# A two-layer graph network on one core: attention outputs made turned, and node degrees laid a target a partition by way of DRAM

## The chip, the core and the metric

The kernel runs on one core of one Trainium2 chip. The metric is device time in microseconds (us) of one execution. The core has a matrix engine (PE, whose weight loads are listed apart as PEld), a vector engine (DVE), a scalar engine (ACT), a general engine (POOL) and a queue engine (SP) that issues most of the transfers; each works through its own instructions in order, and semaphores hold one engine until another has done its part.

## The reference

There are 1250 nodes of 512 features and 20000 edges, sorted by target. Two layers, both added to `x`:

```python
h = relu(layernorm(x))
x = x + L0(h, edges)      # below
h = relu(layernorm(x))
x = x + L1(h, edges)      # sum over neighbours, two dense products with batch norm and relu

def L0(x, edges):
    xn   = batchnorm(x)
    agg  = segment_sum(xn[src], dst) / max(deg, 1)[:, None]
    conv = relu(agg @ W_conv + b_conv)
    q, k, v = heads(x @ Wq), heads(x @ Wk), heads(x @ Wv)   # the first 256 nodes, 8 heads of 64
    qf, kf = phi(q), phi(k)                                 # 256 exponential features each
    kv = kf.T @ v
    z  = 1 / (qf @ kf.sum(nodes) + 1e-6)
    attn = (qf @ kv) * z @ Wo
    return batchnorm(conv + attn[pos] + x)
```

Only the first 256 nodes have attention rows of their own; later nodes take the last one's.

## The kernel before

`tile_gnn` (L1439 on) first makes, from the sorted edges, the keys by which the adjacency matrix can be counted; then `sorted_graph` does both layers. (A second program, `any_graph`, serves unsorted edges and does not run on these inputs.)

**The opening, L1458 to L1609.** Every instruction here goes through `order(...)`, which pins it to the place where it is written. Two transfers bring the targets (`kd`, rows of 400 edges that overlap, a new row every 160) and the sources (`ks`). DVE takes a sample of `kd` (L1533) and compares it (`less`, L1528); PE sums that (`cnt`, L1538). DVE makes `begin` and `pick` (L1561, L1528). PE then picks the edges of each group of ten targets: 20 small matmuls from `ks16` and 20 from `kd16` (L1568), all into one PSUM tile `keys`. Around these `keep_up` (L1517) issues matmuls on zeros whose result nobody reads: six before `cnt`, three before the 40. `halved` (L1543) makes f16 copies of `kd` and `ks` on ACT. After the 40, DVE makes `js`, `prow` and `kcol` (L1606 to L1608), each 128x250, and ACT copies `ed.dist` (L1609).

**Layer 0, in `sorted_graph`.** The 25 `batch` steps count the adjacency matrix: `onehots` (L206) makes two one-hot tiles on DVE, `op` and `ok`, `count` multiplies them on PE (L217), ACT copies the result into `adj` (L220). Most of these instructions are not pinned: a scheduler places them by their data, so what stands late in the text may run early. While the batches are made, `beside` turns the nodes (L226), makes keys (L245), their scores (L267), their maxima on DVE (`kmx`, L334, folded into `km` and turned by PE at L352), values (L337), queries (L245 again), and on DVE the statistics `gst` (L325) and the first two normalised tiles `xn` (L289).

Then comes a loop of ten iterations (L493 to L509). Iteration i issues `query(i)`: scores on PE (L267), row maxima on DVE (L461), exponentials on ACT (L465), scale on DVE (L466). Then `product(i)`: normalised nodes times `W_conv` (L422, 8 PE instructions of 512 columns), with `hi` and `lo` halves made by ACT (L110) and DVE (L111). In iterations 2 to 7 `degrees` follows: a one-hot of 21 groups on DVE (L431), two matmuls with ones that put the degree of 210 targets on all 128 partitions (L435), a maximum and a reciprocal on DVE (L437, L438) into `rdeg`, which lies in the memory of a weight that is no longer needed. Then one `batch`; `turn(i-1)`, which transposes query features (L472) with an ACT copy (L474); and `attend(i-2)`: for two heads and two blocks of 128 features a matmul with the query features as weights and 65 columns of `kv` moving, 64 value columns and one of key sums (L482). DVE adds a constant to the key sums (L485), takes the reciprocal (L486) and scales the two heads (L489) into `ao`, nodes on partitions.

After the loop `ao` is transposed on PE (L514) with four ACT copies (L516) into `aT`, features on partitions, and multiplied by `Wo` (L521). Then the aggregation (L575) multiplies `hi` and `lo` by `adj`; DVE multiplies each result by `rdeg` (L578).

**The end of the program** is the second layer: the neighbour sum (L707), two dense products (L764) and the output.

Of the kernel before, what the change touches and what calls it, by code (L numbers as in the profile page):

```python
# [11 lines left out]
F32 = mybir.dt.float32  # L12
F16 = mybir.dt.float16
F32R = mybir.dt.float32r
I32 = mybir.dt.int32
I16 = mybir.dt.int16
AF = mybir.ActivationFunctionType
# [20 lines left out]
S = 128  # L38
# [31 lines left out]
def sorted_graph(ctx: ExitStack, tc: tile.TileContext, ed, x, n1g, n1b, n2g, n2b, wconv, bconv,  # L70
# [354 lines left out]

    rdeg = ed.wk.rearrange("p k n -> p (k n)")[:, :N]

    def degrees(g0, n):
        shape = [128, n, TG, 2]
        oh = tmp.tile(shape, F16, name="oh", tag="row")  # L430
        nc.vector.tensor_tensor(oh, ed.iok[:, :TG, :].unsqueeze(1).to_broadcast(shape),  # L431
                                ed.dist[:, g0:g0 + n].unsqueeze(2).to_broadcast(shape), ALU.is_equal)
        ps = mm.tile([128, n * TG], F32, name="mm")
        for i in range(2):
            nc.tensor.matmul(ps, ed.ones, oh[:, :, :, i].rearrange("p g t -> p (g t)"), start=(i == 0), stop=(i == 1))  # L435
        c = slice(g0 * TG, (g0 + n) * TG)
        nc.vector.tensor_scalar(rdeg[:, c], ps, 1.0, None, op0=ALU.max)  # L437
        nc.vector.reciprocal(rdeg[:, c], rdeg[:, c])  # L438

    kv = ap1.tile([128, 2, HEADS, DH + 1], F32, name="kv")  # L440
    ao = ap1.tile([128, NT, HEADS, DH], F32, name="ao")
# [34 lines left out]
    def attend(n):  # L476
        t, b = pairs[n]
        pa = mm.tile([128, 2, DH + 1], F32, name="mm")
        for i in range(2):
            hd = 2 * b + i  # L480
            for mb in range(2):
                nc.tensor.matmul(pa[:, i, :], qfTs[n][:, i, mb, :], kv[:, mb, hd, :],  # L482
                                 start=(mb == 0), stop=(mb == 1))
        z = ap2.tile([128, 2], F32, name="z")
        nc.vector.tensor_scalar(z, pa[:, :, DH], KEPS, None, op0=ALU.add)  # L485
        nc.vector.reciprocal(z, z)  # L486
        for i in range(2):
            hd = 2 * b + i
            nc.vector.tensor_scalar(ao[:, t, hd, :], pa[:, i, :DH], z[:, i:i + 1], None, op0=ALU.mult)  # L489
# [3 lines left out]
    for i in range(len(pairs) + 2):  # L493
# [7 lines left out]
        if 2 <= i < 8:  # L501
            degrees(21 * (i - 2), min(21, NGR - 21 * (i - 2)))
# [7 lines left out]
    aT = ap1.tile([128, KD, TOK], F32, name="aT", tag="tT")  # L510
    for f in range(KD):
        ps = mm.tile([128, TOK], F32, name="mm")
        for t in range(NT):
            nc.tensor.transpose(ps[:, t * 128:(t + 1) * 128],  # L514
                                ao[:, t, 2 * f:2 * f + 2, :].rearrange("p h d -> p (h d)"), ident)
        nc.scalar.copy(aT[:, f, :], ps)  # L516
# [467 lines left out]
def any_graph(ctx: ExitStack, tc: tile.TileContext, ed, x, src, dst, n1g, n1b, n2g, n2b, wconv, bconv,  # L984
# [8 lines left out]
    ident = const.tile([128, 128], F32)  # L993
    make_identity(nc, ident)
    ones = const.tile([128, 128], F32)
    nc.vector.memset(ones, 1.0)
    epsc = const.tile([128, 1], F32)
    nc.vector.memset(epsc, EPS)
# [440 lines left out]
def tile_gnn(ctx: ExitStack, tc: tile.TileContext, x, src, dst, *rest):  # L1439
# [11 lines left out]
    ed.dist = pre.tile([128, NGR, 2], I16, name="dist")  # L1451
# [6 lines left out]
    with tc.tile_pool(name="raw", bufs=1) as raw, tc.tile_pool(name="rawp", bufs=1, space=PSUM, side="right") as rawp:  # L1458

        kd, ks = (raw.tile([KS, SPAN], I32, name=name) for name in ("kd", "ks"))  # L1460
        kd16, ks16 = (raw.tile([KP, SPAN], F16, name=name) for name in ("kd16", "ks16"))
        few = E - (KP - 1) * STEP * RB

        def edges(queue, t, v, p0, p1, c0, c1):
            at = bass.AP(tensor=v.tensor, offset=v.offset + p0 * STEP * RB + c0, ap=[[STEP * RB, p1 - p0], [1, c1 - c0]])
            order(queue.dma_start(t[p0:p1, c0:c1], at))

        edges(nc.sync, kd, dst, 0, 112, 0, SPAN)
        edges(nc.scalar, kd, dst, 112, KS, 0, STEP * RB)
        edges(nc.scalar, kd, dst, 112, KP, STEP * RB, few)  # L1470
        edges(nc.scalar, kd, dst, 112, KP - 1, few, SPAN)
# [47 lines left out]
        keep_up(6)  # L1519
# [20 lines left out]
        def halved(t, t32, scale):  # L1540
# [105 lines left out]
```

## Time and profile before

| | |
|---|---|
| median of 3 runs | 375.6 us (373.75 to 375.77) |
| the profiled execution: its own time | 375.39 us |
| the profiled execution: span from first to last instruction | 373.6 us |
| busy PE / DVE / ACT / POOL | 356.9 / 235.8 / 157.0 / 35.4 us |

The chain that ended last passes the stages at these times: opening 0 to 12 us; keys, scores and queries 12 to 63; the loop 63 to 127; transposes and `Wo` 127 to 135; aggregation 135 to 182; layer norm 182 to 193; neighbour sum 193 to 241; dense products and output 241 to 373.

How to read it: an engine's busy share says how full it is, not whether it holds the end up. The chain of waits says that: it is followed back from the last instruction, at each step to what released it. A timeline row gives start, length, engine, source line, operation, the tiles written and read, partitions and columns, and how many equal instructions it stands for. PE rows count instructions: an f32 product is two of them.

### The profile page before, as it was taken

Reading aid. Unit: us, or ns where it says so; the run is one execution under the profiler, and the core shown is the slowest. Engines: PE = TensorE matmul, PEld = TensorE weight load, DVE = VectorE, ACT = ScalarE, POOL = GpSimd, SP = SyncE. Lnnn points to the kernel's source line nnn. Section 1 sums busy time; section 2 is a strip of 40 time slices with the busy share of each in tenths; the row PEclk is TensorE's granted clock in tenths of the full one; section 3 lists DMA queues with packets and bytes.
Section 4 is the critical chain, followed back from the end, with each engine's and each line's share of the span. In section 5 each row is a group of like instructions: output and inputs, shape, how many; then the busy total and the mean of one; then the engine's idle time right before and its main releaser. Section 6 shows DMA issues by size and latency. Waiting matters only on the chain.

```text
span 373.6 us, 4916 instructions
## 1 busy us (share of the span) xinstructions
PE 356.9 (96%) x1840; PEld 262.6 (70%) x1840; DVE 235.8 (63%) x585; ACT 157.0 (42%) x310; POOL 35.4 (9%) x55
## 2 busy tenths in 40 slices
PE   8799979999999999999999999999999999999981
PEld 4665555676565699998768888777777777777761
DVE  6899994648897325677888223172881788414673
ACT  5598549727574360111056503132552552122211
POOL 3100000000000005000000009620053000000000
PEclk9999999999999999999999999999999999999996
DMA  6853020000000372000000000050000000000124
GB/s 209 277 185 118 11 103 0 0 3 2 0 1 2 126 269 105 0 3 0 0 2 0 2 0 1 24 203 0 0 2 1 1 2 0 1 0 11 59 84 130
DMA packets 13285, 18.06 MB, mean 48 GB/s; under 512 B 1341, under 2 KB 6658, under 8 KB 13254
## 3 DMA queue, kind: packets, MB, share of 16 engines
q1 hardware_dynamic: 12542, 17.34, 13.7%
q8 instruction: 16, 0.26, 0.3%
q10 hardware_dynamic: 712, 0.33, 0.3%
q14 instruction: 15, 0.12, 0.1%
HBM read 15.11 MB, written 2.56 MB: 47 GB/s over the span
## 4 chain that ended last, share of the span: by engine, by line
PE 86%; DVE 9%; ACT 2%; DMA 1%; issue 1%; DVEq 0%
PE mm L764 31%; PE mm L707 12%; PE mm L575 12%; PE hw L422 10%; PE mm L245 3%; PE mm L449 2%; PE mm L521 2%; PE mm L482 2%; PE sc L267 2%; PE acc L217 2%; DVE op L206 1%; PE mm L226 1%; PE mm L701 1%; DVE kmx L334 1%; PE mm L472 1%; DVE ok L206 1%
## 5 line engine op out<-in xcount | busy, mean ns | idle before, releaser
L422 PE MATMUL hw<-wconv,xn 128*128 128x512 f32 (+1 forms) x80 | 37.1, 604 | 0.3 <-ACT adj L220 0.3
L779 ACT ACTIVATE kept<-mm,vT 128x313 f32<-128x313 f32 x36 | 18.5, 521 | 42.9 <-PE mm L764 41.8
L707 PE MATMUL mm<-hi,adj 128*128 128x512 f32 (+2 forms) x100 | 32.1, 399 | 0.5 <-DVE hi L655 0.4
L707 PE MATMUL mm<-lo,adj 128*128 128x512 f32 (+2 forms) x100 | 31.6, 394 | 0.0
L129 ACT ACTIVATE r<-mv,epsc 128x1 f32<-128x1 f32 x16 | 4.7, 292 | 61.6 <-DVE mv L128 61.6
L764 PE MATMUL mm<-hid,w 128*128 128x313 f32 x96 | 25.9, 427 | 0.0
L422 PEld LDWEIGHTS hw<-wconv,xn 128*128 128x128 f32 (+1 forms) x80 | 14.1, 187 | 16.4 <-issue 14.8
L575 PE MATMUL mm<-adj,lo 128*128 128x416 f32 (+3 forms) x120 | 25.1, 355 | 0.0
L575 PE MATMUL mm<-adj,hi 128*128 128x416 f32 (+3 forms) x120 | 25.1, 355 | 0.0
L206 DVE TENSOR_TENSOR op<-iop,prow 128x1280 f16<-128x1280 f16 (+2 forms) x27 | 20.7, 768 | 6.0 <-PE acc L217 5.6
L784 DVE TENSOR_TENSOR hid<-mm,kept 128x313 f32<-128x313 f32 x24 | 10.9, 478 | 20.4 <-ACT kept L779 16.9
L764 PEld LDWEIGHTS mm<-hid,w 128*128 128x128 f32 x96 | 18.1, 190 | 6.9
L575 PEld LDWEIGHTS mm<-adj,hi 128*128 128x128 f32 x120 | 21.9, 189 | 1.1
L575 PEld LDWEIGHTS mm<-adj,lo 128*128 128x128 f32 x120 | 21.8, 189 | 1.0
L707 PEld LDWEIGHTS mm<-hi,adj 128*128 128x128 f32 (+2 forms) x100 | 18.4, 186 | 5.8 <-DVE hi L655 1.4
L698 DVE SCALAR_TENSOR_TENSOR z<-h,e,mm 128x512 f32<-128x512 f32 (+1 forms) x10 | 7.0, 744 | 23.5 <-PE mm L707 15.7
L707 PEld LDWEIGHTS mm<-lo,adj 128*128 128x128 f32 (+2 forms) x100 | 18.5, 186 | 4.6 <-DVE lo L648 0.2
L217 PEld LDWEIGHTS <-op 128*128 128x128 f16 x250 | 13.7, 97 | 9.1 <-issue 4.7
L217 PE MATMUL acc<-ok,op 128*128 128x100 f16 x250 | 16.2, 207 | 3.3 <-DVE ok L206 2.7
L702 ACT COPY zT<-mm 128x512 f32<-128x512 f32 (+1 forms) x10 | 5.3, 582 | 29.3 <-PE mm L701 29.3
L764 PE MATMUL mm<-tz,w 128*128 128x313 f32 x64 | 17.5, 426 | 0.0
L764 PE MATMUL mm<-hid,sw 128*128 128x313 f32 x64 | 17.5, 427 | 0.0
(253 smaller groups left out, 704.6 us busy)
## 6 DMA issues: line engine op xcount, KB each, us to landing
w<-in_L_gnn_W_dram SPq DMA_DIRECT2D x2, 2048.0 KB
xs<-in_x_dram SPq DMA_DIRECT2D x1, 2304.0 KB
out_dram<-xs SPq DMA_DIRECT2D x7, 256.0 KB
wk<-in_L_gnn_Wk_dram SPq DMA_DIRECT2D x1, 1024.0 KB
x<-in_x_dram SPq DMA_DIRECT2D x1, 1024.0 KB
v<-in_L_gnn_Wv_dram SPq DMA_DIRECT2D x1, 1024.0 KB
wconv<-in_L_gnn_W_conv_dram SPq DMA_DIRECT2D x1, 1024.0 KB
wk<-in_L_gnn_Wq_dram SPq DMA_DIRECT2D x1, 1024.0 KB
```

What stands on the lines that cost most here:

```text
L206: i = nc.vector.tensor_tensor(t[:, qs], iota.unsqueeze(1).to_broadcast(shape), keys[:, bt, qs].unsqueeze(2).to_broadcast(shape), ALU.is_equal)
L217: nc.tensor.matmul(acc[:, :, q * TG:(q + 1) * TG], op[:, q, :, i], ok[:, q, :, i].rearrange("p (j t) -> p j t", t=TG), start=(q == 0 and i ...
L245: nc.tensor.matmul(ps, wt[:, k, b * 128:(b + 1) * 128], hT[:, k, :TOK], start=(k == 0), stop=(k == KD - 1))
L267: nc.tensor.matmul(ps[:, a, :M], tT[a * 64:a * 64 + 64, b, t * 128:(t + 1) * 128], projT[a * 64:a * 64 + 64, :], start=True, stop=True)
L422: nc.tensor.matmul(ps[:n], xn[:, f, :n], wct[:, f, :], start=(f == 0), stop=(f == KD - 1))
L449: nc.tensor.matmul(ps[:, i, :], kf[:, t, hd, mb * 128:(mb + 1) * 128], va[:, t, hd, :], start=(t == 0), stop=(t == NT - 1))
L482: nc.tensor.matmul(pa[:, i, :], qfTs[n][:, i, mb, :], kv[:, mb, hd, :], start=(mb == 0), stop=(mb == 1))
L575: nc.tensor.matmul(ps, part[:k, j, fs], adj[:k, j, c], start=(part is hi and j == 0), stop=(part is lo and j == NJ - 1))
L707: nc.tensor.matmul(ps[:n], adj[:k, j, t * S:t * S + n], part[:k, j, :], start=(part is hi and j == 0), stop=(part is lo and j == NJ - 1))
L764: order(nc.tensor.matmul(banks[i], left[:, k, m * 128:(m + 1) * 128], right[:, k, i * NH:(i + 1) * NH], start=(p in (1, 2, 5) and k == 0), ...
L779: nc.scalar.activation(t[:, c, :], self.A[c], AF.Identity, bias=self.part(i, 0, c)[1], scale=1.0)
L784: order(nc.vector.tensor_tensor(self.part(i, j, c)[0], self.B[c], t[:, c, :], ALU.add))
```

## The change

**Attention.** `attend` exchanges the operands. `kv` (64 columns) is the weight and the turned query features (128 columns) move, so that the result has features on partitions. The first head of a pair goes to partitions 0 to 63, the second to 64 to 127, that is, each to a half of the array's columns. The key sums get a matmul of their own for each head, with their one column repeated 64 times as weights. So there are 8 products a pair where there were 4. DVE's addition, reciprocal and scaling are now 128x128 and write `aT` directly; the transposes and copies after the loop are gone.

**Degrees.** The one-hot is the weight now and a column of ones moves: 120 targets come out on 120 partitions, one column a block, 11 blocks in three calls (iterations 2 to 4). The maxima are small, and there is a single reciprocal of 128x11. Two transfers write the 1250 values to a row in DRAM, four bytes each, and a third reads the row back onto all partitions as `rdeg`. `dist` is made again on DVE from `js` and `kcol`; the ACT copy is gone.

**The opening.** The targets come in two transfers, the first 160 columns and the 240 ahead of them, on each queue; `halved` has a third piece; the PSUM tile `keys` is two tiles; `keep_up` issues 7 and 4 instead of 6 and 3.

```diff
     rdeg = ed.wk.rearrange("p k n -> p (k n)")[:, :N]
+    dist = ap1.tile([128, NGR, 2], I16, name="dist")
+    DG = 128 // TG
+    DB = -(-NGR // DG)
+    deg = ap1.tile([128, DB], F32, name="deg")
...
+    row = dram.tile([1, N], F32, name="row")
+    nc.gpsimd.memset(deg, 1.0)
...
+        if b0 == 0:
+            nc.vector.scalar_tensor_tensor(dist, ed.js, -float(JK), ed.kcol, op0=ALU.mult, op1=ALU.add)
...
-        for i in range(2):
-            nc.tensor.matmul(ps, ed.ones, oh[:, :, :, i].rearrange("p g t -> p (g t)"), start=(i == 0), stop=(i == 1))
-        c = slice(g0 * TG, (g0 + n) * TG)
-        nc.vector.tensor_scalar(rdeg[:, c], ps, 1.0, None, op0=ALU.max)
-        nc.vector.reciprocal(rdeg[:, c], rdeg[:, c])
+        ps = mm.tile([128, n], F32, name="mm")
+        for b in range(n):
+            h0, h1 = b * DG, min((b + 1) * DG, g1 - g0)
+            w = (h1 - h0) * TG
+            for i in range(2):
+                nc.tensor.matmul(ps[:w, b:b + 1], oh[:, h0:h1, :, i].rearrange("p g t -> p (g t)"), ed.ones[:, :1],
+                                 start=(i == 0), stop=(i == 1), skip_group_check=True)
...
+        if b0 + n == DB:
+            nc.vector.reciprocal(deg, deg)
+            full, some = DG * TG, NGR // DG
+            end = full * some
+            nc.sync.dma_start(row[0, :end].rearrange("(k p) -> p k", p=full), deg[:full, :some])
+            nc.sync.dma_start(row[0, end:].rearrange("(k p) -> p k", k=1), deg[:N - end, some:])
+            nc.sync.dma_start(rdeg, row[:, :].to_broadcast([128, N]))
...
     def attend(n):
         t, b = pairs[n]
-        pa = mm.tile([128, 2, DH + 1], F32, name="mm")
-        for i in range(2):
-            hd = 2 * b + i
+        pa = mm.tile([128, 2, 128], F32, name="mm")
+        for c in range(2):
             for mb in range(2):
-                nc.tensor.matmul(pa[:, i, :], qfTs[n][:, i, mb, :], kv[:, mb, hd, :],
-                                 start=(mb == 0), stop=(mb == 1))
-        z = ap2.tile([128, 2], F32, name="z")
-        nc.vector.tensor_scalar(z, pa[:, :, DH], KEPS, None, op0=ALU.add)
+                for i in range(2):
+                    w = kv[:, mb, 2 * b + i, :DH] if c == 0 else kv[:, mb, 2 * b + i, DH:].to_broadcast([128, DH])
+                    order(nc.tensor.matmul(pa[i * DH:(i + 1) * DH, c, :], w, qfTs[n][:, i, mb, :],
+                                           start=(mb == 0), stop=(mb == 1), skip_group_check=True))
+        z = ap2.tile([128, 128], F32, name="z")
+        nc.vector.tensor_scalar(z, pa[:, 1, :], KEPS, None, op0=ALU.add)
         nc.vector.reciprocal(z, z)
-        for i in range(2):
-            hd = 2 * b + i
-            nc.vector.tensor_scalar(ao[:, t, hd, :], pa[:, i, :DH], z[:, i:i + 1], None, op0=ALU.mult)
+        nc.vector.tensor_tensor(aT[:, b, t * 128:(t + 1) * 128], pa[:, 0, :], z, ALU.mult)
...
-        if 2 <= i < 8:
-            degrees(21 * (i - 2), min(21, NGR - 21 * (i - 2)))
+        if 2 <= i < 5:
+            degrees(4 * (i - 2), min(4, DB - 4 * (i - 2)))
...
-    aT = ap1.tile([128, KD, TOK], F32, name="aT", tag="tT")
-    for f in range(KD):
-        ps = mm.tile([128, TOK], F32, name="mm")
-        for t in range(NT):
-            nc.tensor.transpose(ps[:, t * 128:(t + 1) * 128],
-                                ao[:, t, 2 * f:2 * f + 2, :].rearrange("p h d -> p (h d)"), ident)
-        nc.scalar.copy(aT[:, f, :], ps)
...
-        edges(nc.sync, kd, dst, 0, 112, 0, SPAN)
-        edges(nc.scalar, kd, dst, 112, KS, 0, STEP * RB)
-        edges(nc.scalar, kd, dst, 112, KP, STEP * RB, few)
-        edges(nc.scalar, kd, dst, 112, KP - 1, few, SPAN)
+        edges(nc.sync, kd, dst, 0, 112, 0, own)
+        edges(nc.scalar, kd, dst, 112, KS, 0, own)
+        edges(nc.sync, ahead, dst, 0, 112, own, SPAN, own)
+        edges(nc.scalar, ahead, dst, 112, KP, own, few, own)
+        edges(nc.scalar, ahead, dst, 112, KP - 1, few, SPAN, own)
...
-        keep_up(6)
+        keep_up(7)
...
-        halved(kd16, kd, 1.0)
+        halved(kd16, kd, slice(0, own), 1.0)
+        halved(kd16, ahead[:, :few - own], slice(own, few), 1.0)
+        halved(kd16, ahead[:, few - own:], slice(few, SPAN), 1.0)
...
-        keys = rawp.tile([128, 2, 2, NGR], F32, name="keys")
-        order(nc.tensor.matmul(keys, ed.ones[0:1, :], lead, start=True, stop=False, skip_group_check=True))
-        keep_up(3)
+        keys = [rawp.tile([128, 2, NGR], F32, name=f"keys{kind}") for kind in range(2)]
+        for kind in range(2):
+            order(nc.tensor.matmul(keys[kind], ed.ones[0:1, :], lead[:, kind], start=True, stop=False,
+                                   skip_group_check=True))
+        keep_up(4)
...
-        order(nc.scalar.copy(ed.dist, dist))
```

## The prediction, made before the changed kernel ran

> **What bounds the kernel now.** I read the page's busy times first, then the chain of waits in order of time, then the timeline of single stretches. The page says that PE is busy nearly throughout and that it carries most of the chain that ended last:
>
> ```profile
> span 373.6 us, 4916 instructions
> PE 356.9 (96%) x1840; PEld 262.6 (70%) x1840; DVE 235.8 (63%) x585; ACT 157.0 (42%) x310; POOL 35.4 (9%) x55
> PE 86%; DVE 9%; ACT 2%; DMA 1%; issue 1%; DVEq 0%
> ```
>
> So an edit counts where it changes PE's work, or where the 9% of DVE stand. The chain shows both kinds of place:
>
> ```profile
> 6.33 1.39 PE idle L1517 x3
> 7.73 2.98 PE keys L1568 x40
> 10.74 0.43 DVE js L1606
> 11.19 0.43 DVE prow L1607
> ...
> 37.79 0.38 DVE oh L431
> ...
> 51.97 0.61 DVE kmx L334
> 52.72 0.70 PE sc L267 x4
> ...
> 84.13 0.19 PE mm L435 x2
> ...
> 84.77 0.45 PE mm L472 x4
> 85.22 0.84 PE mm L482 x8
> 86.07 0.63 PE sc L267 x4
> 86.70 3.63 PE hw L422 x8
> ...
> 127.13 0.66 PE mm L514 x6
> 127.81 0.33 PE mm L514
> 128.14 0.65 PE mm L521 x2
> 128.90 6.48 PE mm L521 x30
> ```
>
> The reader sees four stretches: an opening in which PE and DVE alternate; 37.8 to 52.7, where DVE holds the chain (one-hots, `kmx`, statistics); the loop, PE alone, 6.2 us an iteration; and a short turn after it. DVE in the loop is the vector work that the change removes or widens:
>
> ```profile
> 85.53 1.46 DVE L438 RECIPROCAL wk<-wk 128x210 f32<-128x210 f32 x1
> 87.52 0.15 DVE L486 RECIPROCAL z<-z 128x2 f32<-128x2 f32 x1
> 88.31 0.47 DVE L489 TENSOR_SCALAR ao<-mm,z 128x64 f32<-128x64 f32 x2
> ```
>
> And the one place where two parts of the array are used by two products, the scores; a narrow window around 86.0 shows two matmuls that begin together:
>
> ```profile
> 86.00 0.49 PE L267 MATMUL sc<-projT,qT 64*128 64x256 f32 x2
> ```
>
> **The change, part by part.** All sums are made against the profiled execution, 373.6 us of span and 1.8 around it, 375.4; the median of the runs is 0.2 above that.
>
> *Opening.* `js` and `prow` now need only the first of two PSUM tiles and can run beside the 20 matmuls on `kd`; `kcol` can then follow the 40 at once, at about 10.75 and not at 11.52, where the timeline has it: -0.8. The first transfer carries 112x160 numbers and not 112x400, 105 KB less; at the 277 GB/s of the page's second slice that is 0.4 earlier, or nothing if the small transfer on ACT's queue lands last; I take -0.3. One more matmul on zeros stands before the 40; these are 0.43 apart (+0.43). The seventh before `cnt` fills a hole: six end at about 3.9, `cnt` begins at 4.48. That matters for speed: of two equal groups of 20 matmuls the first takes 1.9 (7.52 to 9.40), the second 1.1, so PE's rate doubles near 9.1, after it has been busy with hardly a hole since 4.48. If it doubles before 6.6, the 40 take 40 x 0.057 = 2.3 from `pick`'s end (6.87 less 0.3) to 8.9, and DVE's own order (statistics of `x0` to 9.16 less 0.3, then `js`, `prow`) puts `kcol` at 9.75: -1.8. If the turn stays, the three terms make -0.7. I take -1.5, nearer the first since the hole is filled; ends -1.9 and -0.3. The queue: SP issues one more transfer (0.4) ahead of `ks`, `x0` and `wk`. `x0`'s statistics end 1.5 before `js` today; `wk` is first multiplied at 15.4 and the transfers of 5 to 9 us fall off after 9. Nothing for that.
>
> *12 to 63.* As built, `dist` (like `js`, 128x250: 0.42) is early on DVE; DVE's 0.38 wait for PE at 26.25 absorbs it. The one-hots of `degrees`, scheduled at 37 today, are 960 wide and not 420. Between 420 (0.37) and `ok` of 1000 (0.67) that is 0.65, +0.28 each; the first falls into DVE's 0.35 wait before 37.79, the second does not. In the new order two more `xn` (0.26 each) stand ahead of `km`, for whose transposition (L352) PE waits, and the first scores of the queries are split in two. That is +0.28 + 0.52 + about 0.2 at 53; later ten counting matmuls (0.46) have moved ahead and the 0.26 wait for `adj` before L422 goes, against a second drain for the split scores (0.6). Net +0.8; ends 0 (this stretch gives way elsewhere) and +1.2.
>
> *Loop, attention.* Today 8 instructions in 0.84. Now 16, each with 128 moving columns; transposes of that width (L472) are 0.109 apart. If the halves run together as the scores do, 8 x 0.109 = 0.87, and a change of the array's shape: four score instructions take 0.63 where two steps of 0.216 (L521) are 0.43, so 0.2 for it. 1.05 against 0.84, +0.2 a pair, **+1.6**. If they run one after the other: 16 x 0.109 + 0.2 = 1.94, +8.8. Ends: +0.2 (no cost of the shape) and +8.8. I take the first kind since the only row with two products in parts of the array shows them side by side.
>
> The Trainium skill (TensorEngine Tiling (Array Packing), Key Properties) says that a change of tiling mode, not of tile, drains the engine. The trace agrees: the two 8-column instructions of L248 take 0.53 in the chain where full ones take 0.43. With a drain that costs nothing the whole sum would be 1.4 lower.
>
> *Loop, degrees.* Gone: 6 x 0.19 = 1.1 of PE. New: 22 matmuls of one column, each behind an f16 weight load of 120 columns. Loads of 128 f16 columns keep pace with matmuls 0.046 apart (L217); f32 ones hold L482 at 0.112. Neither has 120 columns, so the middle, 0.075: 1.65, **+0.5**; ends -0.1 and +1.3.
>
> The Trainium skill (TensorE: Matmul & The Clock Gate, Weight-path perf modes) has fast loading only for exactly 128 weights, and 1/1.2 ns a column otherwise; 120 columns would then take 100 ns, an estimate by that page, and the term would be +1.1, the whole 0.6 higher. No row here shows such a load.
>
> *Loop, DVE.* Per iteration 0.38 + 0.37 + 1.46 go in six of them. 0.10 + 0.15 + 0.47 become 0.34 + 0.95 + 0.34 (0.34 is `xn`, 128x128; 0.95 from 1.46 for 210 and 0.15 for 2). The new order holds `qf`, which waits for ACT's exponential, ahead of the next one-hots, so DVE stands some 1.1 in that wait: 5.0 of work and 1.1 make 6.1 of PE's 6.2. What waits for DVE there is the next `product`, for `lo`, with about 1.1 in hand. Nothing, but the cover is thin; without it 0.2 an iteration.
>
> *Degrees by DRAM.* The three transfers start at about 98 on SP; the first reader is L578 at 139.2. The nearest row for small packets is queue 10 on the page: 712 packets in 0.3% of 16 engines' span, 25 ns each. 1250 even through one engine are 31 us, and 640 KB at the 182 GB/s of 120 to 140 another 3.5. Covered. `xs`, next on SP, goes at 125.8 as before. POOL sets `deg` once; it is idle from 40 to 140.
>
> *After the loop.* From the last `attend` to L575 8.05 pass. Now 32 x 0.216 = 6.9, 0.2 for the shape, and a wait: the last `aT` comes 0.3 + 0.95 + 0.3 after the last product lands, while PE has six instructions that do not need it: about 0.35. **-0.6**. The four ACT copies lay on this path and are in that.
>
> Sum: -1.5 + 0.8 + 1.6 + 0.5 - 0.6 = +0.8. Time 376.1.
>
> **The rivals.**
> - *Halves one after the other* (slower). For it: 128-row products share all rows, and no row here shows two column halves. Against it: the scores. +8.8 in place of +1.6: **383.3**. It decides from the point where a pair costs 1.2.
> - *Halves together, their weight loads not hidden.* An f32 load of 64 columns, half of what holds L482 at 0.112, adds 0.055 to each step: 8 x 0.164 + 0.2 = 1.5, +5.4 in all: **379.9**.
> - *DVE's order bounds the loop*: 7 x 0.2 more, **377.5**; the sign is `lo` late for L422.
> - *Faster*: the opening's best end, the middle stretch free, 0.12 a pair, loads of 0.046, a shorter wait before `Wo`: -1.9 + 0 + 1.0 - 0.1 - 0.8 = -1.8, **373.6**. For it: DVE has 5 us of idle time after 56.5 to give back. Against it: L352 waits for DVE before that.
> - *The DRAM row late*: L578 waits, yet seven PSUM tiles stand before PE must stop. 377 and up.
>
> **How the numbers follow.** Forecast 0.42 (own range 374.0 to 377.5), one after the other 0.20, loads not hidden 0.13, DVE's order 0.08, DRAM 0.02, faster 0.15. The likeliest is 376.1. The range 373.4 to 383.5 reaches from the faster case to the serial one and leaves about half of the ends of these two, 0.15, outside. Half a percent (1.9 us) is what a measurement of this kernel can tell: faster 0.15, same 0.42, slower 0.43.
>
> **What would show it.** In the profile after: the new attention products, 16 instructions in about 1.05, with starts in twos; 22 one-column matmuls and their spacing; `kcol` near 10; L352 at 52.9 (53.4 - 1.5 + 1.0); `Wo` in 7.4. The forecast is wrong if the products start one by one 0.109 apart, if PE's rate turns after 9, or if L422 waits for DVE in the loop.

## The result, and the profile after

The changed kernel took **376.78 us** (median of 22 executions, 374.62 to 380.71), the kernel before 374.55 us (22 executions beside it, 373.06 to 376.68). The ratio is **1.0053, with a 95% interval of 1.0032 to 1.0075**: slower by half a percent, 2.0 us. Three of the 22, at 380.3 to 380.7, are left out of the ratio as disturbed; they are named here because three more, at 379.8 to 380.1, belong to the same group, and what makes that group is part of the answer.

The profiled execution took 377.19 us, 1.8 more than that of before. The page after, busy times, the shares of the chain and the loop's `product`:

```profile
span 375.4 us, 5038 instructions
PE 359.2 (96%) x1909; PEld 262.8 (70%) x1909; DVE 233.6 (62%) x568; ACT 155.2 (41%) x306; POOL 35.7 (10%) x56
PE 84%; DVE 9%; ACT 2%; DMA 2%; SPq 1%; issue 1%; DVEq 0%
L422 PE MATMUL hw<-wconv,xn 128*128 128x512 f32 (+1 forms) x80 | 37.2, 606 | 0.0
```

PE has 2.3 us more of work, DVE 2.2 less, and the shares of the chain are nearly what they were. The last line answers one question of the prediction at once: `hw` (L422) stood idle for nothing, so DVE's order in the loop did not hold up the products.

Where the time went is seen in the chain of waits of the changed kernel (start, length, engine, what):

```profile
1.19 3.17 PE idle L1539 x7
...
35.18 0.57 DVE oh L444
35.88 0.66 DVE oh L444
...
46.16 1.54 DVE xn L289 x6
...
48.43 0.61 DVE kmx L334
49.18 1.14 PE sc L267 x4
50.31 1.78 PE acc L217 x20
...
53.05 0.20 PE mm L352
...
67.73 1.23 DVE kf L378
69.00 0.43 PE mm L477 x2
...
128.91 7.10 PE mm L543 x32
136.01 19.08 PE mm L597 x100
...
366.35 2.33 PE mm L913 x10
```

The same chain of before has at these places:

```profile
53.42 0.20 PE mm L352
...
80.50 3.63 PE hw L422 x8
...
135.37 19.07 PE mm L575 x100
...
367.40 0.68 DVE xs L904
```

Read against these lines, and against the timelines of DVE: the opening is 2 us ahead. `kcol` starts at 9.40 where it was 11.52, and the first one-hot `oh` at 35.10 where it was at 37.01. At `km` (L352) only 0.4 of that is left, 53.05 for 53.42. The loop starts level: the first `product` after the keys' values is at 80.44 for 80.50. The loop then takes 1.84 more, most of it eight times 0.18 of attention, and the turn after it 1.14 less, which leaves the aggregation 0.64 late (136.01 for 135.37). That shift is carried to 362 us unchanged. The last 14 us add as much again, `xs` ending the chain at 368.70 for 367.40, and the last 0.5 of the 1.8 comes behind `xs`.

So up to the aggregation most places moved nearly as forecast, and one, between 35 and 69, swallowed more. What stands there is DVE work before `kmx`, and a second thing that the chain does not name: four scores (L267) take 1.14 at 49.18, where four took 0.70 before, and twenty counting products 1.78 where ten take 0.46. Stretches of the same execution show why (us, busy time and instructions of each engine, granted clock, DMA share, GB/s):

```profile
core 0: us, PE busy (x) PEld busy (x) DVE busy (x) ACT busy (x) POOL busy (x), PEclk, DMA share, GB/s
45.89:49.31 3.42, 1.84 (x26) 1.24 (x25) 3.42 (x10) 1.55 (x3) 0.00 (x0) 1.00 0.49 191
49.31:52.72 3.41, 3.41 (x26) 2.42 (x26) 3.38 (x7) 2.28 (x5) 0.00 (x0) 0.50 0.02 5
```

and those of the kernel before at the like place:

```profile
46.67:50.08 3.41, 2.96 (x32) 1.96 (x31) 3.41 (x8) 1.56 (x3) 0.00 (x0) 1.00 0.73 278
50.08:53.49 3.41, 1.99 (x20) 1.14 (x21) 3.41 (x8) 1.87 (x5) 0.00 (x0) 1.00 0.00 0
```

The column PEclk is the granted clock. In the changed kernel it is 0.50 for 3.41 us, right behind 3.42 us in which PE was busy for 1.84; before, 1.99 of 3.41 were enough to keep it. PE waits there for `kmx`, behind six `xn` in a row and an `op`: 1.52 us in one piece (47.66 to 49.18), where before three holes of 0.45, 0.62 and 0.80 stood in the same stretch.

The new products themselves are as the prediction had them. The timeline of the last call of `degrees` and of one pair of `attend` (start, length, engine, line, ..., count):

```profile
97.14 0.48 PE L451 MATMUL mm<-ones,oh 128*120 128x1 f16 x6
...
98.57 1.09 PE L513 MATMUL mm<-qfT,kv 128*64 128x128 f32 x16
```

These six one-column products hold the place for 0.41 (the counting products start at 97.55), the eight of an earlier call for 0.42, and seven of those eight follow each other 0.056 apart. The 16 of `attend` start in twos, 7 ns apart, the twos 0.109 apart, and occupy 1.02.

### The profile page after: what moved, and what is told of

Its sections match the earlier page's. It is cut to its first block, busy times and chain, and to the rows that moved or that the text cites. A ratio compares the mean times of both kernels' runs of the same rounds, so it can differ in the third digit from the quotient of the medians.

```text
span 375.4 us, 5038 instructions
## 1 busy us (share of the span) xinstructions
PE 359.2 (96%) x1909; PEld 262.8 (70%) x1909; DVE 233.6 (62%) x568; ACT 155.2 (41%) x306; POOL 35.7 (10%) x56
## 4 chain that ended last, share of the span: by engine, by line
PE 84%; DVE 9%; ACT 2%; DMA 2%; SPq 1%; issue 1%; DVEq 0%
PE mm L786 31%; PE mm L729 12%; PE mm L597 12%; PE hw L422 9%; PE mm L245 3%; PE mm L513 2%; PE acc L217 2%; PE mm L543 2%; PE sc L267 2%; PE mm L477 2%; DMA x<-in_x_dram 2%; PE mm L913 1%; ACT kf L376 1%; DVE op L206 1%; PE mm L723 1%; PE mm L226 1%
## 5 line engine op out<-in xcount | busy, mean ns | idle before, releaser
L422 PE MATMUL hw<-wconv,xn 128*128 128x512 f32 (+1 forms) x80 | 37.2, 606 | 0.0
L422 PEld LDWEIGHTS hw<-wconv,xn 128*128 128x128 f32 (+1 forms) x80 | 14.1, 187 | 16.8 <-issue 15.4
L786 PE MATMUL mm<-zT,w 128*128 128x313 f32 x64 | 17.4, 427 | 0.0
```

The lines of the kernel that those rows point to most:

```text
L422: nc.tensor.matmul(ps[:n], xn[:, f, :n], wct[:, f, :], start=(f == 0), stop=(f == KD - 1))
L786: order(nc.tensor.matmul(banks[i], left[:, k, m * 128:(m + 1) * 128], right[:, k, i * NH:(i + 1) * NH], start=(p in (1, 2, 5) and k == 0), ...
```

## The experiments

The first theory: the parts add up, the opening is worth 1.9, and the loss sits between 35 and 69 us, where the degrees' one-hots stand ahead of `kmx` and PE's long wait lets the clock fall. The rivals: attention is dearer than its products, the degrees are dear in their products or in DRAM, or the opening's gain is lost whatever else is done. Every edit below is to the kernel named; the kernel before ran beside each on the same chip, and ratios are to it.

### Each part alone

**The opening alone.** The kernel before with the changed opening; the rest is as before.

```diff
-        edges(nc.sync, kd, dst, 0, 112, 0, SPAN)
+        edges(nc.sync, kd, dst, 0, 112, 0, own)
...
+        edges(nc.sync, ahead, dst, 0, 112, own, SPAN, own)
...
-        keep_up(6)
+        keep_up(7)
...
-        keys = rawp.tile([128, 2, 2, NGR], F32, name="keys")
+        keys = [rawp.tile([128, 2, NGR], F32, name=f"keys{kind}") for kind in range(2)]
```

> The kernel before with the opening of the change alone: the split transfer of dst, two key tiles, the seventh and the tenth matmul on zeros; attention, one-hots and degrees are those of before. Theory A (the parts add, and what the opening gains is kept as long as PE is not made to idle later): PE's rate doubles near 4.9, kcol ends near 9.8, L352 stands near 51.5 (53.4 - 1.9) and the whole is 1.9 us faster, 372.7 against 374.6. Rival B (the later transfers or the clock give it back, whatever the other parts do): kcol near 9.8 as well, but L352 not before 52.9, with PE at half clock somewhere between 47 and 53, and the whole is at most 0.6 faster.

Measured: 374.19 against 374.94, ratio 0.9974 (0.9948 to 1.0001). The profiled execution shows both theories at work one after the other. `kcol` starts at 9.88 and the first scores of the queries at 51.40 where they were at 52.72: 1.3 ahead (its rate doubles only at 7.13 in this execution). Then the clock falls:

```profile
48.09:51.51 3.42, 1.56 (x19) 0.93 (x17) 3.42 (x6) 2.54 (x6) 0.00 (x0) 1.00 0.07 25
51.51:54.92 3.41, 3.41 (x11) 2.30 (x12) 3.03 (x8) 0.00 (x0) 0.00 (x0) 0.50 0.02 5
```

and the aggregation starts at 135.68, 0.3 later than before. This execution took 376.36. Five of the twelve, those with a mean granted clock of 0.992 or more, took 372.8 to 373.6, 1.3 to 2.1 less than the median of before; the three with 0.983 or less took 376.0 to 377.1. The five lie below each of the 29 executions of before (the lowest took 373.76). So the opening's gain is there in some executions, and the traced one, in which the clock falls, has given it back. The opening's edits (transfers, key tiles, matmuls on zeros) were not tried one by one.

**Attention alone.**

```diff
-    ao = ap1.tile([128, NT, HEADS, DH], F32, name="ao")
+    aT = ap1.tile([128, KD, TOK], F32, name="aT")
...
+                for i in range(2):
+                    w = kv[:, mb, 2 * b + i, :DH] if c == 0 else kv[:, mb, 2 * b + i, DH:].to_broadcast([128, DH])
...
-            nc.tensor.transpose(ps[:, t * 128:(t + 1) * 128],
```

> The kernel before with the attention of the change alone (turned outputs, halves, replicated key sums, no transposition after the loop). Theory A: 16 products in 1.02 where 8 took 0.84, eight times, +1.45, and -0.6 after the loop: +0.8, 375.4 against 374.6; up to 53 us nothing moves. Rival B (the loss of the change lies in attention and is larger than its products show, by DVE's order in the loop): +2 or more, with L422 waiting for DVE's lo.

Measured: 374.91 against 374.94, 0.9992 (0.9969 to 1.0015). The chain has each pair at 1.02 and the turn after the loop at 7.10:

```profile
123.00 1.02 PE mm L485 x16
...
129.11 7.10 PE mm L514 x32
136.21 19.06 PE mm L568 x100
```

The aggregation starts 0.84 late, of which 0.3 are a rate that doubled 0.6 later in this execution. The trace thus says about +0.5 and the times -0.3 with 0.9 either way; +0.8 is just outside. Rival B is out: attention is not where the change lost.

**Degrees alone**, with `dist` copied in the opening as before.

```diff
-        if 2 <= i < 8:
-            degrees(21 * (i - 2), min(21, NGR - 21 * (i - 2)))
+        if 2 <= i < 5:
+            degrees(4 * (i - 2), min(4, DB - 4 * (i - 2)))
```

> The kernel before with the degrees of the change alone (one-hots of 32 groups, 22 one-column products, the row by DRAM), but dist copied in the opening as before. Theory A: 22 products 0.05 apart are 1.1 in place of 6 x 0.19 = 1.14, so nothing in the loop; two one-hots of 0.66 in place of 0.38 stand ahead of L352, +0.3 to +0.6 at 53 us, with PE idle longer before it: 375.0 against 374.6. Rival B (the longer idle time of PE makes the clock fall): a granted clock of 0.5 for some 3 us near 50, and +1.5 or more. Rival C (small packets or the row by DRAM cost something later): L600 or L422 waits for a DMA.

Measured: 377.41 against 374.94, 1.0056 (1.0031 to 1.0081), +2.1. That is as much as the whole change loses. It isn't the clock's fall near 50 here: the traced execution has none, and it took 377.12. The chain:

```profile
48.27 1.54 DVE xn L289 x6
...
50.55 0.60 DVE kmx L334
...
54.47 0.20 PE mm L352
...
69.15 1.23 DVE kf L378
70.42 0.44 PE mm L474 x2
...
136.84 19.06 PE mm L600 x100
```

L352 is 1.05 later than before, 0.2 of it by an opening in which the rate doubled 0.5 later. A second delay follows: DVE's order now has `op`, which waits for PE, ahead of the second scale of `kf` (L378), so that this starts 2.2 later than before and L474 waits for it. The loop's products then start 1.36 late. Inside the loop the degrees add 0.1; the aggregation is 1.47 late. Rival C is out: nothing waits for a DMA, and the multiplication by `rdeg` does not hold the aggregation. The price of the degrees is paid before a single one of them is computed, by where a scheduler puts their one-hots and what else it then moves.

### Halves one after the other

The changed kernel with the loop over the halves put outermost.

```diff
-        for c in range(2):
-            for mb in range(2):
-                for i in range(2):
+        for i in range(2):
+            for c in range(2):
+                for mb in range(2):
```

> The changed kernel with the loop over the two halves put outermost in attend: the same 16 products, but those of one half follow each other, so that two neighbours share their columns in all but one place. Theory A (two halves of the columns work at once only where neighbours differ): a pair takes 8 x 2 x 0.109 = 1.75 less one overlap, 1.6 to 1.75 in place of 1.02, eight times: +4.6 to +5.8, 381.5 to 382.5 against 376.8 for the changed kernel. Rival B (what a pair takes is the sum of its weight loads, 0.055 each by half of 0.112, whatever their order): no difference, 376.8.

Measured: 381.6 (4 executions), 1.0168 (1.0135 to 1.0202), 4.3 more than the changed kernel. A pair took 1.51 (101.32 to 102.83, where the next scores start):

```profile
101.32 1.58 PE L513 MATMUL mm<-qfT,kv 128*64 128x128 f32 x16
```

Nearer to theory A: the same 16 products in another order cost 0.49 more a pair. But 1.51 lies below its 1.6 to 1.75, and the starts in the trace show that its picture, one overlap in all, isn't right. The eight products of a half stand 0.109 apart as they did, and those of the second half begin with the fifth of the first, 0.49 after the pair's first, and run between the rest: 0.49 and 1.02 make 1.51. It is so in all eight pairs. So halves that are grouped still overlap, by half of their length, and the forecast's 1.05 hung on the innermost loop being the one over halves.

### Where the one-hots stand, and the old degrees

**The changed kernel with late one-hots.** `dist` gets memory that the queries' squares hold until about 61 us, so no one-hot can be made before.

```diff
-    dist = ap1.tile([128, NGR, 2], I16, name="dist")
+    dist = ap2.tile([128, NGR, 2], I16, name="dist", tag="sq")
```

> The changed kernel with one line different: dist is given the memory that the squares of the queries use, so that dist and the two one-hots of the degrees cannot be made before about 61 us, and no longer stand on DVE between 35 and 37, ahead of kmx. Theory A (the new degrees cost what they cost through where their one-hots stand, 2 x 0.66 ahead of the keys' maxima, and through the longer idle time of PE that follows, in which the clock falls in some executions): L352 starts near 51.7 where it was at 52.98, and the whole is 1.5 to 2.5 faster than the changed kernel, 374.3 to 375.3 against 376.8. Rival B (their price lies in the products, in the row by DRAM or in the loop's DVE): L352 moves, but the whole stays above 376.3.

Measured: 375.02 against 375.31, **1.0000** (0.9978 to 1.0023), from 1.0053. One line takes the whole loss away by the ratio, and the two intervals don't meet. In L352 it shows: 52.03, though the rate doubled 1.5 later in this execution than in that of the changed kernel. PE's wait is three holes again (0.45, 0.62, 0.79). The two traces themselves differ by less than the times: here too the clock falls for one step, from 50.84 on, where it makes eight products of L245 take 2.91 and not 1.89, and of the 0.95 at L352 0.20 is left at the aggregation (135.81 for 136.01). Rival B, that the products or the DRAM row cost it, is out. One of the twelve executions took 1275.25 us; it is not in the ratio, no trace of it was kept, and its cause is not known.

**The changed kernel with the degrees of before** (six calls, `ed.dist` by ACT).

```diff
-        if 2 <= i < 5:
-            degrees(4 * (i - 2), min(4, DB - 4 * (i - 2)))
+        if 2 <= i < 8:
+            degrees(21 * (i - 2), min(21, NGR - 21 * (i - 2)))
```

> The changed kernel with the degrees of before (six calls of 21 groups, the degrees made on all partitions at once, six reciprocals, no DRAM); opening and attention stay changed. Theory A (the parts add: opening -0.75 and attention 0.0 as measured alone): 374.0 to 374.4 against 376.8 for the changed kernel, so that the degrees are worth +2.4 within the change as they are alone. Rival B (the sum of the parts exceeds them, by the clock): 375 or more.

Measured: 374.58 against 375.31, 0.9996 (0.9968 to 1.0024); opening and attention alone, multiplied, would give 0.9966, which lies just outside, so the sum of the parts is not borne out to better than 1 us. The median lies between theory A's 374.0 to 374.4 and rival B's 375 or more. What the trace gives is the cleanest ledger of the case, since the clock did not fall near 50 in it. PE around 50:

```profile
48.11 0.70 PE L267 MATMUL sc<-projT,kT 64*128 64x256 f32 x4 [0.44 <-DVE kmx L334]
49.43 0.63 PE L217 MATMUL acc<-ok,op 128*128 128x100 f16 x10 [0.62 <-DVE ok L206]
50.85 0.70 PE L267 MATMUL sc<-projT,qT 64*128 64x256 f32 x4 [0.80 <-DVE kmx L334]
51.49 0.27 PE L352 MATMUL mm<-ident,km 128*8 128x128 f32 x1
```

The last scores of the keys start at 48.11 where the changed kernel has 49.18 (1.07), L352 at 51.49 for 52.98 (1.49, so the half clock adds 0.42), the first products of the loop 1.82 earlier (so 0.33 more, where the scale of `kf` is late), the aggregation at 134.05 for 136.01 (1.96). Against the kernel before, the opening's 1.96 at `kcol` is 1.87 at 80 us: kept whole.

**The same with late one-hots**, to compare old and new degrees with DVE's order equal up to `dist`.

```diff
+    dist = ap2.tile([128, NGR, 2], I16, name="dist", tag="sq")
...
+        if g0 == 0:
+            nc.vector.scalar_tensor_tensor(dist, ed.js, -float(JK), ed.kcol, op0=ALU.mult, op1=ALU.add)
```

> The same with the late dist of the run with late one-hots: old degrees, changed opening and attention, one-hots not before 61 us. DVE's order is then the same as in that run up to dist, so the two differ by the degrees alone. Theory A (in the loop the new degrees cost nothing, 22 x 0.05 in place of 6 x 0.19, and the DRAM row is hidden): both within 0.6 us of each other, 373.5 to 374.8, and both faster than before. Rival B (the new degrees save DVE 1.46 in six iterations, and so time): the late new degrees are faster by 0.6 or more. Rival C (they cost PE or DMA something that the traces do not name): slower by 0.6 or more.

Measured: 374.22 against 375.31, 0.9981 (0.9958 to 1.0003). The late new degrees are at 1.0000: 0.7 us apart, with intervals that overlap by most of their width. Rival B is out; between A and C the times don't decide. The traces favour A: the aggregation starts at 135.81 with the new and 136.09 with the old, both with one fall of the clock, the latter with its rate doubled 0.75 later. The degrees' own price, where their one-hots do no harm, is about nothing.

### The clock

**Filling PE's wait.** Sixteen matmuls on zeros, four behind each of four batches.

```diff
-            batch(next(batches))
+            op = batch(next(batches))
+            if 12 <= piece < 17:
+                spare = mm.tile([S, 512], F32, name="mm")
+                for _ in range(4):
+                    nc.tensor.matmul(spare, op[:, 0, :, 0], ed.zeros, start=True, stop=True)
```

> The changed kernel with 16 matmuls on zeros more, four behind the counting of each of four batches between 40 and 52 us, where PE waits for DVE; they wait for the same one-hots as the counting does, and nobody reads them. Theory A (a 3.41 us window in which PE is busy less than about 0.56 makes the clock fall for one or two windows, and this befalls about half of the executions of the changed kernel): no record of 0.5 between 45 and 60, no execution above 379, median 0.8 to 1.5 lower than the changed kernel's, 375.3 to 376.0. Rival B (the clock is not what makes the spread): executions above 379 stay, the median is 376.8 or more, by up to 16 x 0.216 = 3.5 if the matmuls find no idle time.

Measured: 380.54, 1.0145 (1.0116 to 1.0174): some 3.5 slower than the changed kernel. As a test of what the fall costs it failed. The scheduler put three of the four groups behind L352, where PE was busy anyway (the first of them below), and left the wait open:

```profile
51.42 0.67 PE L267 MATMUL sc<-projT,qT 64*128 64x256 f32 x2 [1.47 <-DVE kmx L334]
...
52.13 1.03 PE L413 MATMUL mm<-zeros,op 128*128 128x512 f16 x4
```

The 3.5 are what rival B gave as its most, 16 times 0.216. Near 50 the trace agrees with the windows: the clock did not fall there, the least busy window between 40 and 60 having 0.57, and the six executions lie within 1.6 us of each other (379.8 to 381.4), none in a group of its own.

**The changed kernel twice more**, for two further traces of the same instructions in the same order.

> The changed kernel once more, for a second trace of the same instructions in the same order. Theory A (the clock is set by windows of 3.41 us whose places change from execution to execution, and a window falls when PE is busy less than about 0.56 of it): if a window of the grid lies so that PE's idle time of 1.5 us near 48 is split between two windows, there is no record of 0.5 before 360, L245 behind L352 takes 1.9 a block and not 2.9, and the loop starts some 1.5 us earlier than in the trace at hand, less 0.5 for each us that the first record of 1.0 comes later; if not, one or two windows of 0.5 follow. Rival B (the clock falls by something in the program that is the same in each execution): the record of 0.5 again 44.4 us after the first of 1.0.

> The changed kernel a third time, for the same reading at another place of the windows; expectations as for the run before. An execution with two windows of 0.5 should stand near 380, one with a single window near 377, one with none near 375.5.

Measured: 378.82 and 377.02. Neither trace is without a fall, so the first expectation of theory A was not met; but they show one and two. The first of them, in steps of 3.41:

```profile
47.88:51.30 3.42, 1.71 (x24) 1.10 (x21) 3.42 (x7) 2.01 (x5) 0.00 (x0) 1.00 0.03 11
51.30:54.71 3.41, 3.04 (x15) 2.14 (x16) 2.51 (x7) 1.52 (x4) 0.00 (x0) 0.50 0.02 5
54.71:58.12 3.41, 3.41 (x9) 1.76 (x7) 1.65 (x3) 0.50 (x2) 0.00 (x0) 0.50 0.00 0
```

and PE behind L352 in it:

```profile
53.93 3.62 PE L245 MATMUL mm<-hT,wk 128*128 128x256 f32 x8
```

Two steps at half clock: eight products of L245 take 3.62, in the first trace 1.89. The loop starts 2.88 later than in the first trace, 0.67 of it already there at the last scores of the keys, since the rate doubled 2.0 later; the execution is 1.6 longer, its clock falling at the end only when PE had nothing left to do. In the other execution the rate doubles at 4.75 and falls at 49.12 for one step, as in the first trace; it took 377.02.

In all fourteen traces of this study, of twelve different kernels, the steps count from the first doubling, which is the first record of a granted clock in the trace: a fall near 50, where there is one, begins 13 steps of 3.413 after it (44.37). That this number is the same, as rival B had it, is no evidence against windows, since PE's wait stands at much the same place in all these kernels; what speaks for them is which traces have a fall. The eight windows of the grid that precede one have PE busy for 0.45 to 0.54 of it; the lowest window between 40 and 60 us of each of the other six has 0.57 to 0.61, and among those is the run with the old degrees, which has the same three holes as the opening alone. There the grid divides the holes between two windows (2.07 of 3.41 in the first); in the opening alone it does not (1.56). The place of the grid changes from execution to execution: the changed kernel's first doubling is at 4.93, 6.92 and 4.75 in three.

Away from 50 us the busy share alone does not decide. All 22 falls of the fourteen traces, the one at the end of each included, follow a window of 0.54 or less, and no window of 0.57 or more is followed by one. But four windows of 0.43 to 0.54 at full clock are followed by none. Two of them, from the second trace of the changed kernel and from the run with 16 matmuls on zeros:

```profile
365.32:368.73 3.41, 1.45 (x11) 0.95 (x9) 2.80 (x11) 0.41 (x2) 0.00 (x0) 1.00 0.41 121
8.84:12.25 3.41, 1.84 (x21) 1.47 (x18) 3.31 (x11) 2.18 (x4) 1.13 (x12) 1.00 0.82 251
```

So a window that is busy for half or less is what a fall needs in these traces, and not always enough for one; what else counts was not settled.

So the executions of the changed kernel seem to be of three kinds. Eleven of the 22 have a mean granted clock of 0.990 or more and took 374.6 to 377.1; one step of half clock, with the shortest slow end of the fourteen traces (4.9 us), would leave 0.989, so these had most likely none; six took 379.8 to 380.7, with 0.978 to 0.983, which fits two steps at half clock; the other five took 376.1 to 377.3. That the six are the two-step kind is inferred from clock and time: their traces were not taken, and the one execution of this kernel that shows two steps took 378.82.

The Trainium skill (TensorE: Matmul & The Clock Gate, What's actually happening) has a free-running window of 3413 ns, and the grid in these traces agrees with it: 3.41 us, another place in each execution. Of the way down the page says that the clock falls after an idle window, and advises (Why this matters for your kernels) against idle gaps of over about 3 us. Here the measurement differs, and decides: in eight traces it fell after a window with 1.6 to 1.9 us of waiting, in one piece or in three, and not after an idle one.

### A version that beats both

**Opening of the change, attention and degrees of before, late one-hots.**

```diff
+    dist = ap2.tile([128, NGR, 2], I16, name="dist", tag="sq")
...
-        order(nc.scalar.copy(ed.dist, dist))
```

> A version that may beat both: the changed opening, the attention and the degrees of before, with dist made late as in the run with late one-hots. Theory A: the opening's gain (-0.75 alone) and up to 2 x 0.38 of DVE ahead of the keys' maxima: 0.994 to 0.997 of the kernel before, 373.2 against 375.0. Rival B (one-hots of 420 columns are absorbed by DVE's other waits, as L352 of the two runs with old degrees suggests): 0.9975, as the opening alone.

Measured: 374.5 against 375.85, 0.9981 (0.9955 to 1.0008). Nearer to rival B: 420-column one-hots ahead of the keys' maxima cost nothing that moving them brings back. In its trace the clock falls (0.52 of a window).

**The same with two f32 products more in PE's wait.**

```diff
+            if n == 6:
+                spare = mm.tile([128, M], F32, name="mm")
+                for _ in range(2):
+                    nc.tensor.matmul(spare, kf[:, t, o, :128], kf[:, t, o, :], start=True, stop=True)
```

> The same with two f32 matmuls of 256 columns more on PE, behind the copy of the seventh pair of key scores and ahead of the eighth pair, in the time near 48 in which PE waits for DVE; nobody reads them. They reorder DVE and PE between 48 and 66 a little. Theory A (the clock falls in a quarter of the executions of the kernels with this hole, at 1.7 to 3 us each, and a filled hole spares it): no execution with a clock share under 0.986, the highest execution within 2 us of the lowest, 0.3 to 0.6 lower than the run before in the mean. Rival B (the new order costs more than the clock brings): 0.5 or more above it.

Measured: **373.95 against 375.85, 0.9962 (0.9941 to 0.9983)**, faster than the kernel before and than the changed one, and the twelve executions lie within 1.4 us (373.1 to 374.5), the narrowest of all here. The filler stands in the wait:

```profile
45.54 0.70 PE L267 MATMUL sc<-projT,kT 64*128 64x256 f32 x4 [0.85 <-DVE kmx L334]
46.87 0.40 PE L217 MATMUL acc<-ok,op 128*128 128x100 f16 x5 [0.62 <-ACT kf L333]
47.10 1.09 PE L343 MATMUL mm<-kf 128*128 128x256 f32 x4
```

and the least busy window between 40 and 60 has 1.94 of 3.41 (0.57), with no fall. The spread and the mean, 0.5 lower than in the run before, are as theory A had them. L352 starts at 50.88, against 51.81 in the run without filler and 53.35 before; the aggregation starts at 133.58. How much of this is the clock and how much the order, which the two products also changed (`km` comes 0.9 earlier), isn't separated: against the run without them the difference is 0.7 us, inside the intervals.

## Why the prediction was right, and where not

The time, 376.1, is within 0.7 of the median, and the sign came out. Part of that nearness is luck. The sum starts from 375.4, the profiled execution of before (with +0.8 it would be 376.2), and the median of before was 374.55 in the result: as a change, +0.8 was forecast and +2.0 measured. In the trace the sum holds up to the aggregation (+0.64), but there errors of both signs cancel. The table is from the run with the old degrees, whose clock did not fall near 50, and the changed kernel:

| step | forecast | measured |
|---|---|---|
| opening | -1.5 (-1.9 to -0.3) | -1.9 |
| 12 to 80, everything but the opening | +0.8 (0 to +1.2) | +1.8 |
| loop, attention | +1.6 | +1.7 |
| loop, degrees on PE | +0.5 (-0.1 to +1.3) | +0.1 |
| after the loop | -0.6 | -1.1 |
| sum | +0.8 | +0.6 |

*Opening.* Right in kind, a little better: the seventh matmul closes the hole, the rate doubles at 4.93, `kcol` starts at 9.40, 2.1 early and just past the better end; in the run with the old degrees 1.87 are left at 80 us. The term is not one number, though. The doubling comes at the end of the first full window, 4.75 to 7.22 in the traces with this opening and 9.12 to 9.74 in those without it.

*12 to 80* is the step that failed: its size by a factor of two, and outside its ends. L352 came at 52.98, forecast 52.9, but two errors met there. DVE's order cost 1.07 up to the last scores of the keys, close to the "+0.28 + 0.52 + about 0.2" of the step. On top came the half clock, 0.42 in this trace and some 2.2 more in another (2.88 less the 0.67 that stood before it), a term that the working did not have. And the "net" after 53 had the wrong sign: the `op` put ahead of the scale of `kf` costs 0.33 in the changed kernel where the step had -0.2. The step did say what to look for, two more `xn` ahead of `km`; it added their lengths and did not ask what PE would do in one long wait where there had been three short ones.

*Attention in the loop* is right in its parts: starts in twos, 8 x 0.109 and 0.15 for the change of shape, 1.02 forecast as 1.05. What the loop takes beyond eight times 0.18 lies in the last two iterations, where no scores stand between `attend` and `hw`: there `hw` takes 3.63 and 3.60 where it took 3.49 and 3.46. The serial run shows that the order decides, but not that the rival's picture was right: even grouped by half the products overlap, a pair takes 1.51, and the price is +5.4 by that number and not +8.8. The rival with unhidden weight loads is out.

*Degrees on PE.* The spacing was taken at 0.075 and is 0.056, nearer the lower bound, that of loads of 128 f16 columns (0.046). A load of 120 columns lasts 0.134 in the trace where one of 128 lasts 0.097, so the narrower loads are the slower ones; but they overlap, and little of it is seen in the spacing.

The rule of the Trainium skill that the prediction weighed (TensorE: Matmul & The Clock Gate, Weight-path perf modes, with the rate from LDWEIGHTS (loading the stationary operand)) would have made the spacing 0.100, an estimate from that page; the measured 0.056 decides.

*Degrees by DRAM*, *DVE in the loop* and *the queue*, each costed at nothing: no wait for `rdeg`, none of `hw` for DVE, none for `xs`. Covered as said. The rival "DVE's order bounds the loop" was wrong of the loop; DVE's order did cost, between 35 and 53 us.

*After the loop.* 7.10 and not 7.4: the wait for the last `aT` is nearly hidden. In the chain of before the stretch took 8.24, so the gain is 1.1; the 8.05 of the working go from start to start, by which the new stretch is 6.82.

What is left between +0.64 and the +1.8 of the two profiled executions is the end of the program. The clock falls at 366.75 there, soon after the last ten transposes have begun (2.33, most of it at half clock), and at 367.52 before, behind them. That makes 0.66 by the last `xs`; the other 0.5, behind `xs`, was not traced to a cause.

```profile
366.75:370.16 3.41, 1.92 (x9) 1.52 (x8) 2.07 (x6) 0.00 (x0) 0.00 (x0) 0.50 0.22 56
```

Where that falls changes with the place of the windows; in the run with attention alone the fall came at 368.14 and cost nothing. The sum of the two traces is therefore no better a measure of the change than the times are.

Still open: how much of the 2.0 us is the order of DVE and how much the clock. The order makes the loss where degrees are alone (+2.1, with no fall near 50 in the trace). In the whole change both take part. The three traces of the changed kernel vary the clock with the order unchanged, but none of them is without a fall. A rough split is in the executions: the eleven with a clock of 0.990 or more have a median of 375.8, 1.2 above that of before, and the rest comes with the others.

## What to carry to other kernels

When a change lengthens or moves work on the engine that feeds PE, ask not only how much later PE's next instruction comes but how much PE then waits within a few microseconds: here a 3.41 us window with PE busy for about half of it was often followed by half the clock for one or two more. Look in the built order for what a scheduler hoists: work for a late stage that has its data early may be put into the tightest stretch of the program, and one line that ties it to a buffer that comes free later takes it out again. And judge such a change by the spread of its executions as well as by one trace.

## What the runs showed that was not expected

- Near 50 us the clock falls for one or two steps of 3.41 us after a window in which PE is busy for 0.54 or less (eight traces), and not where the lowest window has 0.57 or more (six traces). That is 1.6 to 1.9 us of waiting. It is no full rule: elsewhere four windows of 0.43 to 0.54 had no fall behind them.
- To come back it wants a nearly full window: after 0.93, 0.99 and 1.00 it came back, after 0.89 it did not, and in the opening 0.84 and 0.85 were not enough to start it. One trace does not fit: in the run with serial halves PE was busy through the whole window after the fall, by the records, and the clock stayed at half for a second one. A busy PE in the records is not a PE at its peak, so this may be a matter of what counts; it was not settled.
- A kernel changed for the better in its opening can lose the gain again in some executions, by where a later wait falls in the windows: the opening alone took 372.8 to 373.6 in five executions and 376.0 to 377.1 in three, those with the lowest clock.
- Products in two halves of the columns run side by side throughout only when neighbours in the order use different halves: 1.02 for 16 alternating. Grouped by half, the second half's begin with the fifth of the first, and the same 16 take 1.51.
- One-column products behind f16 loads of 120 columns go through 0.056 us apart, though each load lasts 0.134.
